# The query graph's product by seven products of halves in place of eight

## The chip, the cores and the metric

The kernel runs on one core of one Trainium2 chip. The metric is the device time of one execution in microseconds (us). The times given are medians of several executions; the profile comes from one more execution.

## The reference

There are 16 batches of x, each with N = 1024 nodes and C = 256 channels, in float32, and one adjacency matrix of 1024 x 1024 that all batches share. Two layers are computed for each batch. What matters here is the first one:

```python
c_adj = mean over channels of x                     # one number for each node
A     = abs(abs(sigmoid(c_j - c_i) - 0.5) - 0.5) * 2
Wg    = adj * (A + A.T) / 2                         # [N, N], other for each batch
g     = x.T @ Wg                                    # [C, N] = [C, N] @ [N, N]: the query graph's product
q     = relu(g * para)                              # queries
kv    = x @ kv_w                                    # keys and values
out   = softmax(q @ k.T * scale) @ v                # four heads of 64 channels
x     = layernorm(x + out)
```

The second layer is a graph convolution of two steps with the plain `adj` (hidden size 128), added to x with a relu and normalised again.

## The kernel before

The order of the work is written out by hand in `run()`; each engine carries out its own instructions in that order, and semaphores join the engines. Batches are staggered. While the attention of batch b is computed, the second layer of batch b-1 (`conv`) and the preparation of batch b+1 are put between its parts.

The attention of a batch has four units (two pairs of heads, two halves of the nodes). In a unit, `scores` makes eight score tiles on TensorE (L388), ScalarE takes their exponential (L391), VectorE adds the eight up for the denominators (L395, L397), transposes the sum and reduces it (L399, L401). `outputs` multiplies with the values (L408) and VectorE transposes the result to `o` (L412). `add` folds the denominators on TensorE (`den_ps`, L420) and divides and adds on VectorE (L424 to L431).

After unit 0 stands `first` (conv.first on TensorE, loads and transposes of x of the next batch, its means), after unit 1 `second` (conv.second, L550), after unit 2 `last` (conv.last, L557 and L558, with a residual sum on VectorE, L562 and L565). In `first` the hidden nodes go through DRAM (`h1d`, L526 and L528).

The queries of batch b+1 are made by the class `Queries`. A batch has eight tiles of 128 rows of Wg. `load` fetches a tile of adj through SP's queue (L334). `likeness` makes A's tile on ScalarE in two activations (L343, L344). `times_adj` multiplies it by adj on VectorE (L349), which gives `wg`. `step(t)` (L357) multiplies the 128 rows of x by the 128 rows of wg: two blocks of channels (cb) by two halves of the nodes (j), four products of 128x128 by 128x512, accumulated over the eight steps in two PSUM tiles of two banks each. TensorE carries out each such float32 product as two passes, which are what the profile counts. `end` multiplies by `para` on VectorE (L363) and applies relu on ScalarE (L364).

After unit 3 stand the eight steps, with parts of the layer norm of batch b among them (`norm.mean`, L265 and L268; `norm.squares`, L274 and L275; `norm.variance`, L279, with a power on GpSimd, L281). Then follow `end`, `norm.scale` (L286), `norm.spread` (two transposes, L174, and eight writes x1d and one load x1 on SP's queue, L295 and L297), `keys` (L307, two halves with a copy on ScalarE each, L309) and `values` (L319, four pieces with a copy each, L321). Then the next batch's scores begin, and the loads of x (L94) and of xB, x in transposed blocks (L106), follow on SP's queue.

Row tiles of 128x1024 come from one pool of 21 buffers. PSUM has three tiles of two banks ("big": scores, g_ps, k_ps, conv) and two of one bank ("bank": av, den_ps, sums, v_ps).

Batch 0's queries are made ahead of the loop, batch 1's during the attention of batch 0, when there is no conv yet.

Of the kernel before, what the change touches and what calls it, by code (L numbers as in the profile page):

```python
# [10 lines left out]
F32 = mybir.dt.float32  # L11
I32 = mybir.dt.int32
AF = mybir.ActivationFunctionType
# [5 lines left out]
def kernel(  # L19
# [31 lines left out]
    nc = tc.nc  # L51

    B, N, C = x.shape
    P = 128
    NT = N // P
    NC = C // P
# [3 lines left out]
    FB = 512  # L60
# [22 lines left out]
    def big_psum(name):  # L83
        return psum.tile([P, N], F32, tag="big", name=name, bufs=3)
# [4 lines left out]
    def bank_psum(name):  # L89
        return psum.tile([P, FB], F32, tag="bank", name=name, bufs=2)  # L90
# [6 lines left out]
    def row_tile(name):  # L97
        return work.tile([P, N], F32, tag="row", name=name, bufs=ROWS)
# [63 lines left out]
    def adj_blocked(mt):  # L162
        t = row_tile(f"adjB_{mt}")
        for a in range(Q):
            nc.sync.dma_start(
                out=t[a * S:(a + 1) * S, :].rearrange("k (bn r) -> k bn r", r=S),
                in_=adj[:, mt * P + a * S:mt * P + (a + 1) * S].rearrange("(bn k) r -> k bn r", k=S))
        return t
# [88 lines left out]
    class BlockedNorm:  # L257


        def __init__(self, xB, sums, name):  # L260
            self.xB, self.sums, self.name = xB, sums, name
# [37 lines left out]
    def keys(b, xT, between=lambda: None):  # L299
        kT = work.tile([P, NC, N], F32, tag="kT", name=f"kT_{b}")  # L300
        for kb in range(NC):
            if kb == 1:
                between()
            pk = big_psum(f"k_ps_{b}_{kb}")
            for j in range(NJ):
                for cc in range(NC):
                    nc.tensor.matmul(pk[:, ts(j, FB)], kvw_sb[:, cc, ts(kb, P)], xT[:, cc, ts(j, FB)],  # L307
                                     start=(cc == 0), stop=(cc == NC - 1))
            nc.scalar.copy(kT[:, kb, :], pk)  # L309
        return kT  # L310

    def values(b, xT, copy=nc.scalar.copy):
        v = work.tile([P, NT, C], F32, tag="v", name=f"v_{b}")
        per = FB // C
        for g in range(NT // per):
            pv = bank_psum(f"v_ps_{b}_{g}")
            for i in range(per):
                for cc in range(NC):
                    nc.tensor.matmul(pv[:, ts(i, C)], xT[:, cc, ts(g * per + i, P)], kvw_sb[:, cc, C:2 * C],  # L319
                                     start=(cc == 0), stop=(cc == NC - 1))  # L320
            copy(v[:, g * per:(g + 1) * per, :], pv.rearrange("p (i c) -> p i c", c=C))  # L321
        return v

    class Queries:
# [26 lines left out]
        def step(self, t):  # L351
            if t == 0:
                self.pg = [big_psum(f"g_ps_{self.b}_{cb}") for cb in range(NC)]
            wg = self.wg.pop(t)
            for cb in range(NC):
                for j in range(NJ):
                    nc.tensor.matmul(self.pg[cb][:, ts(j, FB)], self.xb[:, t, ts(cb, P)], wg[:, ts(j, FB)],  # L357
                                     start=(t == 0), stop=(t == NT - 1))

        def end(self):  # L360
# [3 lines left out]
                nc.scalar.activation(qT[:, cb, :], qT[:, cb, :], AF.Relu, scale=QSCALE)  # L364
            return qT

    class Attention:


# [235 lines left out]
    def run():  # L605

        xT, c_col = prepare_first(x_first)
        q = Queries(0, x_first)
        for t in range(NT):
            q.load(t)
        load_para()
        blocked = load_blocked(1, "1")
        load_weights()

        def first_weights():  # L620
            q.c_row, q.c_col = first_row(c_col), c_col
            q.weigh(0)

        kT = keys(0, xT, first_weights)
        for t in (1, 2):
            q.likeness(t)
        v = values(0, xT, nc.vector.tensor_copy)
        for t in (1, 2):
            q.times_adj(t)
        xb = load_x(1, "1")  # L630
        tiles = {}

        def turn_adj(mts):
            for mt in mts:
                nc.vector.transpose(adjT_sb[:, mt, :], tiles.pop(mt))

        for t in range(NT):
            if t + 3 < NT:
                q.weigh(t + 3)
            q.step(t)  # L640
            if t == 4:
                xB = load_blocked(0, "a0")
                ready = {}
                ready["xT"], ready["part"] = prepare(blocked, "1")
            if t == 6:
                ready["mean"] = means(ready["part"], "1")
        qT = q.end()
        old = conv = None
        for b in range(B):
            more = b + 1 < B  # L650
            att = Attention(b, xB, qT, kT, v)
            if conv and more:
                xb = load_x(b + 1, str(b + 1))

            def first():
                blocked = load_blocked(b + 1, str(b + 1))
                conv.first(blocks=True)
                if old:
                    old.moments()
                conv.turn_blocks(0)  # L660
                ready["xT"], ready["part"] = prepare(blocked, str(b + 1))
                if old:
                    old.finish(out[b - 2])
                conv.turn_blocks(1)
                att.add(0)
                ready["mean"] = means(ready["part"], str(b + 1))

            def second():
                for t in range(3):
                    q.load(t)  # L670
                conv.second(blocks=True)
                att.add(1)

            def last():
                conv.last()
                att.add(2)

            between = [first, second, last] if conv and more else []
            if more:
                q = Queries(b + 1, xb)  # L680
            for u in range(len(UNITS)):
                att.scores(u)
                if u and not between:
                    att.add(u - 1)
                att.outputs(u)
                if u == 2 and more:
                    q.c_row, q.c_col = ready["mean"]
                    for t in range(3):
                        if not conv:
                            q.load(t)  # L690
                        q.weigh(t)
                if u < 3 and between:
                    between[u]()
            norm = BlockedNorm(xB, att.sums, str(b))
            if more:
                xT = ready["xT"]
                for t in range(3, NT):
                    q.load(t)
                for t in range(3, NT):
                    q.likeness(t)  # L700
                if not conv:
                    for mt in range(0, 4):
                        tiles[mt] = adj_blocked(mt)
                q.times_adj(3)
                q.step(0)
                if conv:
                    att.add(3)
                q.times_adj(4)
                q.step(1)
                if not conv:  # L710
                    att.add(3)
                    turn_adj(range(0, 4))
                    for mt in range(4, NT):
                        tiles[mt] = adj_blocked(mt)
                q.times_adj(5)
                q.step(2)
                q.step(3)
                norm.mean()
                q.times_adj(6)
                q.times_adj(7)  # L720
                q.step(4)
                norm.squares()
                q.step(5)
                q.step(6)
                norm.variance()
                xB = load_blocked(b + 1, f"a{b + 1}")
                q.step(7)
                qT = q.end()
                norm.scale()
                norm.spread()  # L730
                if not conv:
                    turn_adj(range(4, NT))
                kT, v = keys(b + 1, xT), values(b + 1, xT)
            else:
                conv.first(lambda: att.add(3))
                norm.mean()
                norm.squares()
                conv.turn(1)
                conv.neighbours(0)
                norm.variance()  # L740
                conv.neighbours(1)
                norm.scale()
                norm.spread()
                conv.last()
                for k, c in ((b - 2, old), (b - 1, conv)):
                    c.moments()
                    c.finish(out[k])
            old, conv = conv, GraphConv(b, norm.x1, norm.x1T)
        conv.first()
        conv.second()  # L750
        conv.ending(out[B - 1])
# [65 lines left out]
```

## Time and profile before

| what | value |
|---|---|
| median of 10 runs | 2298.79 us (2298.13 to 2299.43) |
| the profiled execution's own time | 2298.55 us |
| its span in the profile | 2296.7 us |
| TensorE busy | 2275.7 us (99%), 8422 passes |
| VectorE busy | 1568.3 us (68%) |
| ScalarE busy | 941.3 us (41%) |
| GpSimd busy | 119.2 us (5%) |
| query graph's passes (L357) | 1024, 598 ns mean |
| distance of the scores of neighbouring batches (579.13 and 720.87 us) | 141.7 us |

The span lies 1.85 us below the execution's own time, which is what the runs measure. Engines: PE is TensorE, DVE is VectorE, ACT is ScalarE, POOL is GpSimd, SP is the engine that issues the transfers. A row of the timeline gives start, duration, engine, line, operation, output and inputs, shape and count; after it, in brackets, the idle time of the engine before it and what ended that. A row of the groups gives line, engine, operation, names, shapes and count, then busy time, mean duration in ns, and the idle time before. TensorE's passes overlap, so that their mean duration (598 ns) is longer than the distance at which they follow each other (0.43 us).

### The profile page before, as it was taken

To read this page: it belongs to the slowest core of one execution; us is meant where nothing else is said; L and a number is where in the kernel's file an instruction comes from. 1 tells how busy PE (TensorE), PEld (TensorE's weight loads), DVE (VectorE), ACT (ScalarE), POOL (GpSimd) and SP (SyncE) were. 2 spreads that over 40 slices of the span, in tenths; PEclk is the share of its full clock that TensorE was granted. 3 is DMA by queue.
4 is the path that set the end of the run, shared out by engine and by line. 5 is a ranking of instruction groups with operands and counts; after the bars stand their busy time and mean duration, and the time that the engine had idled before them with its cause. 6 is when DMAs were issued, how large, how long until landed. Compare 5 with 4: busy or idle time off the path is not lost.

```text
span 2296.7 us, 22441 instructions
## 1 busy us (share of the span) xinstructions
PE 2275.7 (99%) x8422; PEld 1089.5 (47%) x8422; DVE 1568.3 (68%) x2055; ACT 941.3 (41%) x1012; POOL 119.2 (5%) x48
## 2 busy tenths in 40 slices
PE   9999999999999999999999999999999999999997
PEld 4354454544445444454444544445444454444454
DVE  4975767567675766757668576685766867667755
ACT  4733435244352443534425244252542535324420
POOL 0000000100001000010000100001000010000001
PEclk9999999999999999999999999999999999999999
DMA  7391362423524245242342434324343252422102
GB/s 185 91 148 46 67 136 55 83 65 75 128 62 76 66 82 119 65 74 83 73 110 64 79 94 81 87 65 85 99 81 75 65 103 81 87 70 65 37 14 80
DMA packets 568467, 189.37 MB, mean 82 GB/s; under 512 B 487072, under 2 KB 551456, under 8 KB 568352
## 3 DMA queue, kind: packets, MB, share of 16 engines
q1 hardware_dynamic: 568080, 187.35, 37.2%
q8 instruction: 68, 1.11, 0.2%
q10 hardware_dynamic: 272, 0.52, 0.1%
q14 instruction: 47, 0.39, 0.1%
HBM read 146.93 MB, written 40.89 MB: 82 GB/s over the span
## 4 chain that ended last, share of the span: by engine, by line
PE 97%; DVE 1%; DMA 0%; ACT 0%; issue 0%; SPq 0%; POOL 0%; DVEq 0%; ACTq 0%
PE s L388 20%; PE av L408 19%; PE g_ps L357 19%; PE h_ps L514 10%; PE u_ps L550 10%; PE v_ps L319 5%; PE k_ps L307 5%; PE t_ps L500 3%; PE h_ps L512 2%; PE h_ps L557 2%; PE h_ps L558 2%; PE sum_ps L214 0%; PE den_ps L420 0%; PE mean_ps L214 0%; DVE acc L397 0%
## 5 line engine op out<-in xcount | busy, mean ns | idle before, releaser
L391 ACT ACTIVATE pr<-s 128x1024 f32<-128x1024 f32 x512 | 476.1, 1052 | 169.6 <-PE s L388 169.6
L397 DVE TENSOR_TENSOR acc<-acc,pr 128x1024 f32<-128x1024 f32 x384 | 470.5, 1225 | 41.0 <-DVE acc L397 1.4
L388 PE MATMUL s<-qT,kT 64*128 64x512 f32 x2048 | 457.1, 596 | 0.7 <-ACT qT L364 0.7
L357 PE MATMUL g_ps<-wg,x 128*128 128x512 f32 x1024 | 455.1, 598 | 1.1 <-DVE wg L349 1.1
L408 PE MATMUL av<-pr,v 128*64 128x512 f32 x2048 | 453.6, 595 | 0.0
L388 PEld LDWEIGHTS s<-qT,kT 64*128 64x128 f32 x2048 | 191.3, 186 | 225.9 <-ACT pr L391 113.6
L357 PEld LDWEIGHTS g_ps<-wg,x 128*128 128x128 f32 x1024 | 189.6, 190 | 229.2 <-issue 222.3
L408 PEld LDWEIGHTS av<-pr,v 128*64 128x64 f32 x2048 | 141.4, 137 | 300.1 <-issue 261.7
L514 PE MATMUL h_ps<-adjT_sb,t 128*128 128x512 f32 x512 | 224.9, 592 | 0.0
L550 PE MATMUL u_ps<-adjT_sb,h 128*128 128x512 f32 x512 | 224.5, 596 | 0.2 <-ACT h L536 0.2
L395 DVE TENSOR_TENSOR acc<-pr,pr 128x1024 f32<-128x1024 f32 x64 | 78.0, 1219 | 152.0 <-ACT pr L391 152.0
L281 POOL TENSOR_TENSOR rstd<-rstd,neg_half 128x32 f32<-128x32 f32 x16 | 86.9, 5429 | 1680.1 <-DVE rstd L279 1680.1
L550 PEld LDWEIGHTS u_ps<-adjT_sb,h 128*128 128x128 f32 x512 | 95.8, 190 | 126.4 <-issue 125.2
L514 PEld LDWEIGHTS h_ps<-adjT_sb,t 128*128 128x128 f32 x512 | 97.2, 190 | 122.5 <-issue 118.3
L349 DVE SCALAR_TENSOR_TENSOR wg<-wg,adj 128x1024 f32<-128x1024 f32 x128 | 149.5, 1209 | 6.1 <-ACT wg L344 6.1
L343 ACT ACTIVATE wg<-c_row,c_col 128x1024 f32<-128x1024 f32 x128 | 147.2, 1150 | 1.2 <-DVE accB L399 1.2
L424 DVE RECIPROCAL rden<-den_ps 64x16 f32<-64x16 f32 x128 | 31.8, 248 | 156.1 <-PE den_ps L420 155.2
L344 ACT ACTIVATE wg<-wg 128x1024 f32<-128x1024 f32 x128 | 135.4, 1058 | 4.1
L552 ACT COPY uT<-u_ps 128x512 f32<-128x512 f32 x32 | 18.7, 585 | 288.1 <-PE u_ps L550 288.1
L515 ACT ACTIVATE h1T<-h_ps,b_sb 128x512 f32<-128x512 f32 x32 | 22.0, 687 | 247.0 <-PE h_ps L514 247.0
L319 PE MATMUL v_ps<-kvw_sb,xT 128*128 128x256 f32 x512 | 113.1, 379 | 0.0
L307 PE MATMUL k_ps<-xT,kvw_sb 128*128 128x512 f32 x256 | 112.8, 593 | 0.0
(101 smaller groups left out, 1786.7 us busy)
## 6 DMA issues: line engine op xcount, KB each, us to landing
adj<-in_adj_dram SPq DMA_DIRECT2D x128, 512.0 KB, 5.8
xB_a<-in_x_dram SPq DMA_DIRECT2D x128, 128.0 KB, 4.0
x1d<-xB_a SPq DMA_DIRECT2D x128, 128.0 KB, 3.4
x<-x1d SPq DMA_DIRECT2D x16, 1024.0 KB, 5.7
xB<-in_x_dram SPq DMA_DIRECT2D x120, 128.0 KB, 4.6
x<-in_x_dram SPq DMA_DIRECT2D x15, 1024.0 KB, 8.7
out_dram<-x SPq DMA_DIRECT2D x15, 1024.0 KB, 4.7
h1d<-h1B SPq DMA_DIRECT2D x112, 64.0 KB, 2.2
```

The lines of the kernel that those rows point to most:

```text
L307: nc.tensor.matmul(pk[:, ts(j, FB)], kvw_sb[:, cc, ts(kb, P)], xT[:, cc, ts(j, FB)], start=(cc == 0), stop=(cc == NC - 1))
L319: nc.tensor.matmul(pv[:, ts(i, C)], xT[:, cc, ts(g * per + i, P)], kvw_sb[:, cc, C:2 * C], start=(cc == 0), stop=(cc == NC - 1))
L343: nc.scalar.activation(wg, self.c_row, AF.Abs, bias=self.c_col[:, t:t + 1], scale=-1.0)
L344: nc.scalar.activation(wg, wg, AF.Tanh, scale=-0.5)
L349: nc.vector.scalar_tensor_tensor(wg, wg, 1.0, self.adj.pop(t), op0=ALU.add, op1=ALU.mult)
L357: nc.tensor.matmul(self.pg[cb][:, ts(j, FB)], self.xb[:, t, ts(cb, P)], wg[:, ts(j, FB)], start=(t == 0), stop=(t == NT - 1))
L388: nc.tensor.matmul(ps[:, ts(s, FB)], self.kT[rows, pair, ts(mt, P)], self.qT[rows, pair, ts(j, FB)], start=True, stop=True)
L391: nc.scalar.activation(pr, ps, AF.Exp)
L397: nc.vector.tensor_add(acc, acc, pr)
L408: nc.tensor.matmul(pav[s * HD:(s + 1) * HD, :], self.v[:, mt, pair * P + s * HD:pair * P + (s + 1) * HD], self.pr[mt][:, ts(s, FB)], start ...
L514: nc.tensor.matmul(ph, t1[:, mt, :], adjT_sb[:, mt, ts(j, FB)], start=False, stop=(mt == NT - 1))
L550: nc.tensor.matmul(pu, self.h1[:, ts(mt, P)], adjT_sb[:, mt, ts(j, FB)], start=(mt == 0), stop=(mt == NT - 1))
```

## The change

For batches 2 to 15 a new class `FastQueries` makes the product with Strassen's algorithm in the form with 15 additions. x is split into 2 x 2 blocks (two blocks of channels by two halves of the rows), Wg into 2 x 2 blocks (two halves of the rows by two halves of the columns). Seven products of blocks, `p[1]` to `p[7]`, replace eight. They are accumulated over four steps, for each of which two tiles of Wg are needed, k and k+4.

- `left`: four sums of blocks of x, 128x512 each, on GpSimd, in `second`.
- `right(k)`: four sums of blocks of Wg, 128x512 each, on VectorE. `pair(k)` is two `times_adj` and `right(k)`.
- `step(k)`: seven products of 128x128 by 128x512. They accumulate in three big PSUM tiles and one bank.
- `end`: a copy of `p[1]` on ScalarE and seven sums of 128x512 on VectorE, then the multiplications by `para` and the relus as before.

The order around it changes too. Tiles 0 and 4 are loaded and weighted and summed in `second`; tiles 1 and 5 after unit 2; tiles 2, 6, 3 and 7 are loaded and their likenesses made after unit 3's scores. `norm.mean` and `norm.squares` stand in the middle of step 2. `norm.variance` stands between the two halves of the keys, `norm.scale` and `norm.spread` between keys and values. For batches 0 and 1 all stays as it was.

The core of the diff; the branch without a conv (`if more and not conv`) keeps its old order:

```diff
+    class FastQueries(Queries):
...
+        def left(self, eng):
+            s12, s34 = (row_tile(f"S_{self.b}_{k}").rearrange("p (s t c) -> p s t c", s=2, c=P) for k in range(2))
+            eng.tensor_add(s12[:, 0], self.block(1, 0), self.block(1, 1))
+            eng.tensor_sub(s12[:, 1], s12[:, 0], self.block(0, 0))
+            eng.tensor_sub(s34[:, 0], self.block(0, 0), self.block(1, 0))
+            eng.tensor_sub(s34[:, 1], self.block(0, 1), s12[:, 1])
+            self.S = [s12[:, 0], s12[:, 1], s34[:, 0], s34[:, 1]]
...
+        def right(self, k):
...
+            nc.vector.tensor_sub(t12[:, h0], lo[:, h1], lo[:, h0])
+            nc.vector.tensor_sub(lo[:, h1], hi[:, h1], lo[:, h1])
+            nc.vector.tensor_sub(t12[:, h1], hi[:, h1], t12[:, h0])
+            nc.vector.tensor_sub(t4, hi[:, h0], t12[:, h1])
...
+        def pair(self, k):
+            self.times_adj(k)
+            self.times_adj(TJ + k)
+            self.right(k)
...
+        def step(self, k, halfway=None):
+            if k == 0:
+                a, b, c = (big_psum(f"g_ps_{self.b}_{i}") for i in range(3))
+                h0, h1 = ts(0, FB), ts(1, FB)
+                self.p = {1: a[:, h0], 6: a[:, h1], 7: b[:, h0], 5: b[:, h1], 2: c[:, h0], 3: c[:, h1],
+                          4: bank_psum(f"g_ps_{self.b}_3")}
...
+            for n in (1, 6, 2, 7, 4, 5, 3) if k == TJ - 1 else (1, 2, 3, 5, 7, 6, 4):
+                if n == 7 and halfway:
+                    halfway()
+                x_n, w_n = terms[n]
+                nc.tensor.matmul(self.p[n], x_n[:, k, :], w_n, start=(k == 0), stop=(k == TJ - 1))
...
+        def end(self):
...
+            nc.scalar.copy(p1, p[1])
+            add(u[:, h0], p1, p[6])
+            add(qT[:, 0, h0], p1, p[2])
+            add(u[:, h1], u[:, h0], p[7])
+            add(qT[:, 1, h0], u[:, h1], p[4])
+            add(qT[:, 1, h1], u[:, h1], p[5])
+            add(u[:, h0], u[:, h0], p[5])
+            add(qT[:, 0, h1], u[:, h0], p[3])
+            for cb in range(NC):
+                nc.vector.tensor_mul(qT[:, cb, :], qT[:, cb, :], para_sb[:, cb, :])
...
             def second():
-                for t in range(3):
+                q.c_row, q.c_col = ready["mean"]
+                q.left(nc.gpsimd)
+                for t in (0, TJ):
                     q.load(t)
+                    q.likeness(t)
+                q.pair(0)
                 conv.second(blocks=True)
                 att.add(1)
...
                 att.scores(u)
+                if u == 3 and more and conv:
+                    for t in (2, TJ + 2, 3, TJ + 3):
+                        q.load(t)
+                    for t in (2, TJ + 2, 3, TJ + 3):
+                        q.likeness(t)
+                    q.right(1)
...
                 if u == 2 and more:
+                    if conv:
+                        for t in (1, TJ + 1):
                             q.load(t)
+                            q.likeness(t)
+                            q.times_adj(t)
...
+            elif more:
+                xT = ready["xT"]
+                q.pair(2)
+                q.step(0)
+                att.add(3)
+                q.pair(3)
+                q.step(1)
+                q.step(2, lambda: (norm.mean(), norm.squares()))
+                q.step(3)
+                qT = q.end()
+                xB = load_blocked(b + 1, f"a{b + 1}")
+                kT = keys(b + 1, xT, norm.variance)
+                norm.scale()
+                norm.spread()
+                v = values(b + 1, xT)
```

More of the change, by code (lines that the diff above doesn't have):

```diff
@@ L365, in end, with __init__, block @@
             return qT
+    class FastQueries(Queries):
+        def __init__(self, b, xb):
+            super().__init__(b, xb)
+            self.T = {}
+        def block(self, i, j):
+            return self.xb[:, j * TJ:(j + 1) * TJ, ts(i, P)]
+        def left(self, eng):
[6 more added lines that the diff above has]
+        def right(self, k):
+            lo, hi = self.wg[k], self.wg[TJ + k]
+            h0, h1 = ts(0, FB), ts(1, FB)
+            t12 = row_tile(f"T_{self.b}_{k}")
+            if k % 2 == 0:
+                self.t4 = row_tile(f"T4_{self.b}_{k}")
+            t4 = self.t4[:, ts(k % 2, FB)]
+            nc.vector.tensor_sub(t12[:, h0], lo[:, h1], lo[:, h0])
+            nc.vector.tensor_sub(lo[:, h1], hi[:, h1], lo[:, h1])
+            nc.vector.tensor_sub(t12[:, h1], hi[:, h1], t12[:, h0])
+            nc.vector.tensor_sub(t4, hi[:, h0], t12[:, h1])
+            self.T[k] = (t12, t4)
+        def pair(self, k):
[5 more added lines that the diff above has]
+                a, b, c = (big_psum(f"g_ps_{self.b}_{i}") for i in range(3))
+                h0, h1 = ts(0, FB), ts(1, FB)
+                self.p = {1: a[:, h0], 6: a[:, h1], 7: b[:, h0], 5: b[:, h1], 2: c[:, h0], 3: c[:, h1],
+                          4: bank_psum(f"g_ps_{self.b}_3")}
+            lo, hi = self.wg.pop(k), self.wg.pop(TJ + k)
+            t12, t4 = self.T.pop(k)
+            h0, h1 = ts(0, FB), ts(1, FB)
+            terms = {1: (self.block(0, 0), lo[:, h0]), 2: (self.block(0, 1), hi[:, h0]), 3: (self.S[3], hi[:, h1]),
+                     4: (self.block(1, 1), t4), 5: (self.S[0], t12[:, h0]), 6: (self.S[1], t12[:, h1]),
+                     7: (self.S[2], lo[:, h1])}
+            for n in (1, 6, 2, 7, 4, 5, 3) if k == TJ - 1 else (1, 2, 3, 5, 7, 6, 4):
[4 more added lines that the diff above has]
+        def end(self):
+            qT = work.tile([P, NC, N], F32, tag="qT", name=f"qT_{self.b}")
+            u = row_tile(f"U_{self.b}")
+            h0, h1 = ts(0, FB), ts(1, FB)
+            p = self.p
+            add = nc.vector.tensor_add
+            p1 = row_tile(f"P1_{self.b}")[:, h0]
+            nc.scalar.copy(p1, p[1])
[8 more added lines that the diff above has]
+                nc.vector.tensor_mul(qT[:, cb, :], qT[:, cb, :], para_sb[:, cb, :])
+                nc.scalar.activation(qT[:, cb, :], qT[:, cb, :], AF.Relu, scale=QSCALE)
+            return qT
@@ L679, in run @@
             if more:
-                q = Queries(b + 1, xb)
+                q = (FastQueries if conv else Queries)(b + 1, xb)
             for u in range(len(UNITS)):
                 att.scores(u)
+                if u == 3 and more and conv:
[4 more added lines that the diff above has]
+                    q.right(1)
                 if u and not between:
@@ L686, in run @@
                 if u == 2 and more:
-                    q.c_row, q.c_col = ready["mean"]
-                    for t in range(3):
-                        if not conv:
+                    if conv:
+                        for t in (1, TJ + 1):
                             q.load(t)
-                        q.weigh(t)
+                            q.likeness(t)
+                            q.times_adj(t)
+                    else:
+                        q.c_row, q.c_col = ready["mean"]
+                        for t in range(3):
+                            q.load(t)
+                            q.weigh(t)
                 if u < 3 and between:
@@ L694, in run @@
             norm = BlockedNorm(xB, att.sums, str(b))
-            if more:
+            if more and not conv:
                 xT = ready["xT"]
@@ L700, in run @@
                     q.likeness(t)
-                if not conv:
-                    for mt in range(0, 4):
-                        tiles[mt] = adj_blocked(mt)
+                for mt in range(4):
+                    tiles[mt] = adj_blocked(mt)
                 q.times_adj(3)
                 q.step(0)
-                if conv:
-                    att.add(3)
                 q.times_adj(4)
                 q.step(1)
[L710 to L714, printed above, removed]
+                att.add(3)
+                turn_adj(range(4))
+                for mt in range(4, NT):
+                    tiles[mt] = adj_blocked(mt)
                 q.times_adj(5)
@@ L730, in run @@
                 norm.spread()
-                if not conv:
-                    turn_adj(range(4, NT))
+                turn_adj(range(4, NT))
                 kT, v = keys(b + 1, xT), values(b + 1, xT)
+            elif more:
+                xT = ready["xT"]
+                q.pair(2)
+                q.step(0)
+                att.add(3)
+                q.pair(3)
[8 more added lines that the diff above has]
+                v = values(b + 1, xT)
             else:
```

## The prediction

> **What bounds the kernel now.** I read the page's shares first, then the chain that ended last, then the timeline of one of the batches that repeat, TensorE's rows and VectorE's.
>
> ```profile
> span 2296.7 us, 22441 instructions
> ...
> PE 2275.7 (99%) x8422; PEld 1089.5 (47%) x8422; DVE 1568.3 (68%) x2055; ACT 941.3 (41%) x1012; POOL 119.2 (5%) x48
> ...
> PEclk9999999999999999999999999999999999999999
> ```
> ```profile
> PE 97%; DVE 1%; DMA 0%; ACT 0%; issue 0%; SPq 0%; POOL 0%; DVEq 0%; ACTq 0%
> ```
> TensorE is busy all through at a steady clock and carries the chain. Only fewer TensorE passes, or new gaps in them, can move the end. In TensorE's timeline (start, duration, count) the changed product stands between two attentions:
> ```profile
> 529.56 7.09 PE L408 MATMUL av<-pr,v 128*64 128x512 f32 x32
> 536.58 3.70 PE L357 MATMUL g_ps<-wg,x 128*128 128x512 f32 x8
> 540.12 0.30 PE L420 MATMUL den_ps<-den_part,fold 128*128 128x32 f32 x2
> 540.26 10.55 PE L357 MATMUL g_ps<-wg,x 128*128 128x512 f32 x24
> 550.64 0.53 PE L214 MATMUL sum_ps<-sums,fold 128*128 128x32 f32 x4
> 551.00 10.55 PE L357 MATMUL g_ps<-wg,x 128*128 128x512 f32 x24
> 561.39 0.53 PE L214 MATMUL sum_ps<-sq_part,fold 128*128 128x32 f32 x4
> 561.75 3.68 PE L357 MATMUL g_ps<-wg,x 128*128 128x512 f32 x8
> 565.27 7.03 PE L307 MATMUL k_ps<-xT,kvw_sb 128*128 128x512 f32 x16
> ```
> No idle time stands in these rows. Row starts (durations overlap) give 540.26 to 550.64 for 24 passes, 0.4325 us each. A product of halves is two passes, 0.865 us; a batch has 32 products, and the stage takes 28.69 us (536.58 to 565.27). VectorE in that stretch:
> ```profile
> 538.17 1.22 DVE L401 TENSOR_REDUCE den_part<-accB 128x32 f32<-128x1024 f32 x1
> ...
> 551.21 0.19 DVE L265 TENSOR_SCALAR mean<-sum_ps 128x32 f32<-128x32 f32 x1 [5.02 <-PE sum_ps L214]
> ...
> 567.75 2.36 DVE L286 TENSOR_TENSOR xB_a<-xB_a,rstd 128x1024 f32<-128x1024 f32 x2 [1.05 <-POOL rstd L281]
> ```
> VectorE is nearly full in attention but idles 5 us and more here, and its timeline shows 10.25 us of idleness in conv.second and 9.89 us ahead of the next scores. The groups give the prices of the new sums:
> ```profile
> L428 DVE TENSOR_TENSOR o<-o,rden 128x512 f32<-128x512 f32 x64 | 43.8, 684 | 0.0
> L562 DVE TENSOR_TENSOR z<-h2e_ps,b_sb 128x512 f32<-128x512 f32 x4 | 2.7, 686 | 17.4 <-PE h2e_ps L558 17.4
> ```
> From SBUF or with a PSUM operand, a 128x512 sum takes 0.69 us. In the timeline the next one starts 0.73 us later if it depends on the first, 0.63 if not; a weighting (L349) starts each 1.14 us.
>
> [...]
>
> **The change, part by part.** It touches the queries of batches 2 to 15: 14 of 16. I put the batch above on a clock with G = 536.58.
>
> (1) TensorE. 28 products in four steps replace 32 in eight: 4 x 0.865 = 3.46 us off the path per batch, 14 x 3.46 = **48.4 us**. Each product loads its own weights, as before; L550, which also changes weights each time, has 32 passes in 13.83 us (0.432 each), so I charge nothing for the new order. The excess of the old stage, 28.69 - 64 x 0.4322 - three short pieces (0.14, 0.36, 0.36) = 0.17, may go too: 2.4 us more at most.
>
> (2) The right-hand sums: 16 of 0.69 us, four per step. One pair of weightings and its sums is 2.28 + 2.76 = 5.04 us. The first pair moves into conv.second: VectorE is free from 632.3 to 643.0, the sums end at 637.4, 5.6 us to spare. Its two adj transfers stand right behind the h1 load on SP's queue (622.4 before), land in 5.8 us, in time for 632.3. Behind the pair stand the adds of unit 1, which wait for den_ps at 642.9 anyway.
> In unit 2 two weightings replace three: VectorE is 0.95 us ahead in unit 3 (the residual then waits for h2_ps). The second adj there waits for the first attention product of unit 2 (650.8), lands near 656.6 and is wanted at 659.5.
> After unit 3's scores, VectorE: L401 ends G+1.8; the sums of step 1 to 4.5; o to 5.1; pair 2 to 10.2; adds of unit 3 (2.8) to 13.0; pair 3 to 18.0. TensorE: step 0 to 6.05, den_ps, step 1 (6.2 to 12.25), step 2 with the mean after its fourth product (at 15.7, sums ready at 13.0), to 18.7; step 3, second product at 19.5 (its sum ready at 17.4), to **24.7**. The closest is 2.1 us. The eight ScalarE likenesses of tiles 2, 6, 3, 7 now begin when accB frees a buffer, G+0.6, and end by 9.4; VectorE wants them from 5.1 (first done 2.8) to 14.2. Their adj land by G+1.4. So the sums cost nothing; without cover they would cost 14 x 11 = 154 us.
>
> (3) Four left sums on GpSimd: [...]13.5 if an add costs four times the 842 ns of the 128x256 row L139. GpSimd reaches them after its pow of the old norm (600.9) and x's load, VectorE then idles until 606.4, and the product needs them 75 us later. I take 0[...].
>
> (4) The end: seven sums and one ScalarE copy (0.59 us, as L552), then the two multiplications as before. Mean, squares and their sums move ahead of it: VectorE 18.0 to 23.0, first sum to 23.7. The keys start at K = G+24.7 and need only that buffer: 1.0 us of room. By the built program the second sum waits for the last product of its shared buffer, K+0.2; the sums start 0.2, 0.83, 1.56, 2.19, 2.82, 3.55. The second key half waits for the one that starts at 2.82, done 3.5; TensorE arrives at 3.46 + 0.36 = 3.82: room **0.3**. The multiplications end at 6.6, ScalarE's relus 7.7, its key copies 9.7, first value copy 10.3; the third value piece wants it at 10.8: room 0.5. Value taken: 0, up to 1.5 us per batch, 21 us, since three of my spacings are 0.1 us guesses.
>
> (5) Variance moves into the keys. Its 0.36 us on TensorE only moves. VectorE's small operation comes after the multiplications (K+6.6), pow takes 5.43, scale starts K+12.2; scores start K+14.2. Scale and the two transposes end 2.8 us after that, the first accumulation is due at 3.15. The cover, 9.89 us of idleness, is used up. The conv wants x1T 14 us into the scores.
> Behind scale on SP stand the eight x1d writes, the x1 load, the x load, eight xB loads: all move 9.6 us later against the scores. The last xB piece landed 16.1 us after the scores' start (issued 591.0, 4.2 us to land); now 25.7. VectorE transposes it at 29.1 and TensorE needs the mean 2.6 us after VectorE has it: room 3.4 + 2.6 = 6.0 us.
>
> Sum against the profiled execution, 2298.55 (span 2296.7 plus 1.85): 2298.55 - 48.4 = 2250.15. The median, 2298.79, lies 0.24 higher; adding that gives 2250.4, and I say **2250.5 us**.
>
> **Rivals.** (A) As worked out: 2247 to 2257, chance 0.74.
> (B) VectorE's chain or the value copies run late where the room is 0.3 to 1.0 us, and TensorE stalls 1 to 2.5 us per batch. For: VectorE is near full from unit 2 to the end, and sums of different operands have not run in this order. Against: every duration is measured. 1.5 us: 2250.4 + 21 = 2271; up to 2285. Chance 0.17.
> (C) The transfers behind scale become the bound: x1d, x1, x and xB follow one another, and in this trace an xB piece took up to 9.5 us to land. From 6.0 us beyond my plan TensorE waits for the mean, from 9.5 us (6.0 + 3.46) the change loses. At 12 us: 14 x 2.5 = 35, 2334. Against: late xB pieces landed in 4 us and nothing else new loads the queues then. Chance 0.05.
> (D) The saving does not happen: seven products take as long as eight, 0.988 us each, since each needs other weights; 2299. L550 speaks against. Chance 0.04.
>
> **Numbers.** A measurement of this kernel tells about 0.2% from no change (4.6 us). Faster is A, B and a rest of D, 0.92; same 0.03; slower C, 0.05. The range 2247 to 2271 goes from the vanished excess to B's likely size and leaves out the rest of B, C and D.
>
> **What would show it.** Right: 912 g_ps passes beside 1024, still 0.432 us apart; the stage near 24.9 us; scores of neighbouring batches near 138.3 us apart, 141.7 before; VectorE busy about 14 x 23 x 0.69 = 222 us more, ScalarE 8. Wrong: idle time of TensorE ahead of k_ps with U as releaser, of v_ps with the value copy (B), of mean_ps with part (C), or g_ps passes above 0.45 us (D).

## The result and the profile after

The changed kernel took 2252.99 us in the median (2252.2 to 2253.71, 8 runs) beside 2299.14 us for the kernel before (28 runs): 46.15 us less, a ratio of 0.980 with a 95% interval of 0.9791 to 0.9808. The profiled execution took 2252.97 us, with a span of 2251.2 us. The prediction was 2250.5 us, in a range of 2247 to 2271.

The page of the changed kernel, its shares, clock and chain:

```profile
span 2251.2 us, 22596 instructions
...
PE 2229.8 (99%) x8310; PEld 1067.3 (47%) x8310; DVE 1773.9 (79%) x2377; ACT 945.4 (42%) x1026; POOL 188.7 (8%) x104
...
PEclk9999999999999999999999999999999999999999
...
PE 97%; DVE 2%; ACT 0%; DMA 0%; issue 0%; SPq 0%; DVEq 0%; POOL 0%; ACTq 0%
```

TensorE has 112 passes less and 46 us less of busy time, and is still busy for 99% of the span. VectorE has gone from 68% to 79% and the chain still runs through TensorE. At the 0.43 us from start to start that a pass takes in the rows below, 112 passes are 48.1 us: the gain is 2 us short of that.

Now TensorE's timeline of one stage (start, duration, engine, line, operation; line numbers are those of the changed kernel). Step 0 begins at 530.45 and the keys at 555.39:

```profile
530.45 1.98 PE L430 MATMUL g_ps<-wg,x 128*128 128x512 f32 x4
532.27 1.02 PE L430 MATMUL g_ps<-wg,S 128*128 128x512 f32 x2
533.13 1.02 PE L430 MATMUL g_ps<-T,S 128*128 128x512 f32 x2
533.99 1.02 PE L430 MATMUL g_ps<-wg,S 128*128 128x512 f32 x2
534.85 1.02 PE L430 MATMUL g_ps<-T,S 128*128 128x512 f32 x2
535.70 1.02 PE L430 MATMUL g_ps<-T,x 128*128 128x512 f32 x2
536.59 0.41 PE L505 MATMUL den_ps<-den_part,fold 128*128 128x32 f32 x2
536.83 1.96 PE L430 MATMUL g_ps<-wg,x 128*128 128x512 f32 x4
...
555.39 3.60 PE L307 MATMUL k_ps<-xT,kvw_sb 128*128 128x512 f32 x8
558.82 0.53 PE L214 MATMUL sum_ps<-sq_part,fold 128*128 128x32 f32 x4
559.18 3.68 PE L307 MATMUL k_ps<-xT,kvw_sb 128*128 128x512 f32 x8
```

The starts of products lie 0.86 us apart, whichever operands they take; the g_ps groups (L430, and L357 for batches 0 and 1) add up to 912 passes, 1024 before. The stage takes 24.94 us, 28.69 before. From the keys to the next scores (569.70) it is 14.31 us, 13.86 before: the variance's piece of 0.36 us has moved there. Together that is 3.30 us a batch, and 14 x 3.30 = 46.2. The scores of neighbouring batches are 138.4 us apart (unit 2 at 495.04 and 633.47), 141.7 before. One row is new in kind: from den_ps's start to the next it is 0.24 us, 0.14 before. VectorE's rows show why:

```profile
516.33 1.23 DVE L647 TENSOR_TENSOR z<-h_ps,b_sb 128x1024 f32<-128x1024 f32 x1 [0.97 <-PE h_ps L643]
...
532.04 1.22 DVE L486 TENSOR_REDUCE den_part<-accB 128x32 f32<-128x1024 f32 x1
...
535.83 0.71 DVE L497 STREAM_TRANSPOSE o<-av 128x512 f32<-128x512 f32 x1
...
548.47 0.69 DVE L405 TENSOR_TENSOR T<-wg,T 128x512 f32<-128x512 f32 x1
549.08 0.18 DVE L265 TENSOR_SCALAR mean<-sum_ps 128x32 f32<-128x32 f32 x1
...
553.96 0.68 DVE L440 TENSOR_TENSOR U<-P,g_ps 128x512 f32<-128x512 f32 x1
...
558.11 0.68 DVE L445 TENSOR_TENSOR U<-U,g_ps 128x512 f32<-128x512 f32 x1
...
567.56 2.36 DVE L286 TENSOR_TENSOR xB_a<-xB_a,rstd 128x1024 f32<-128x1024 f32 x2 [5.56 <-POOL rstd L281]
```

The transpose to o stands behind the four sums of step 1 and ends at 536.54. den_ps may not begin before: `p[4]` holds one of the two single PSUM banks from step 0 to the end, so den_ps has to write the other one, which is av's, the transpose's source. It starts at 536.59, 0.03 us after step 0's last product lets it. Its weight load, which otherwise runs under that product, had to wait too. In the kernel before the products took no single bank, and the first weight load of den_ps began at 539.69, ahead of the end of the transpose to o (539.31 + 0.70):

```profile
539.69 0.19 PEld L420 LDWEIGHTS den_ps<-den_part,fold 128*128 128x128 f32 x1 [0.24 <-DVE den_part L401]
```

In the changed kernel the list of waits has o (what waited, for what, us in total, times, longest). These are idle times of the weight load, which is busy for only 47% of the span (PEld in the page above); the cost is read from the starts above.

```profile
PEld den_ps L505 <- DVE o L497: 9.7, 14, 0.7
```

The 5 us of VectorE's idleness ahead of the mean are used up, since L405 ends at 549.16 and the mean follows at once; the 10.25 us of idleness in conv.second have become 5.70. The groups give the new sums' prices (busy, mean ns, idle time before):

```profile
L402 DVE TENSOR_TENSOR T<-wg 128x512 f32<-128x512 f32 x56 | 38.3, 683 | 0.0
L440 DVE TENSOR_TENSOR U<-P,g_ps 128x512 f32<-128x512 f32 x14 | 9.5, 678 | 0.0
L389 POOL TENSOR_TENSOR S<-x 128x512 f32<-128x512 f32 x14 | 17.7, 1266 | 25.6 <-PE av L493 25.6
```

### The profile page after: what moved, and what is told of

It reads as the page before. It is cut to its first block, busy times and chain, and to the rows that moved or that the text cites. A ratio compares the mean times of both kernels' runs of the same rounds, so it can differ in the third digit from the quotient of the medians.

```text
span 2251.2 us, 22596 instructions
## 1 busy us (share of the span) xinstructions
PE 2229.8 (99%) x8310; PEld 1067.3 (47%) x8310; DVE 1773.9 (79%) x2377; ACT 945.4 (42%) x1026; POOL 188.7 (8%) x104
## 4 chain that ended last, share of the span: by engine, by line
PE 97%; DVE 2%; ACT 0%; DMA 0%; issue 0%; SPq 0%; DVEq 0%; POOL 0%; ACTq 0%
PE s L473 20%; PE av L493 20%; PE g_ps L430 15%; PE h_ps L599 10%; PE u_ps L635 10%; PE k_ps L307 5%; PE v_ps L319 5%; PE t_ps L585 3%; PE h_ps L597 2%; PE h_ps L642 2%; PE h_ps L643 2%; PE g_ps L357 2%; PE den_ps L505 1%; PE sum_ps L214 1%; PE mean_ps L214 0%; DVE acc L482 0%
## 5 line engine op out<-in xcount | busy, mean ns | idle before, releaser
L430 PE MATMUL g_ps<-wg,S 128*128 128x512 f32 x224 | 115.5, 597 | 0.0
L608 DVE STREAM_TRANSPOSE h1B<-h1T 128x512 f32<-128x512 f32 x28 | 19.9, 712 | 121.0 <-ACT h1T L600 121.0
L430 PE MATMUL g_ps<-T,S 128*128 128x512 f32 x224 | 114.4, 592 | 0.0
L430 PE MATMUL g_ps<-wg,x 128*128 128x512 f32 x224 | 110.2, 604 | 0.0
```

The source lines that it names most:

```text
L430: nc.tensor.matmul(self.p[n], x_n[:, k, :], w_n, start=(k == 0), stop=(k == TJ - 1))
```

## The experiments

Three theories stood to be told apart: the number of products alone sets the gain and all else is hidden (1); the sums or the new order cost time that the products paid back (2); TensorE's products or the borders of its pieces cost something else (3). All kernels derive from the changed one. Times are medians of 4 to 13 runs; the kernel before had 2298.3, 2298.96 and 2298.36 us in the three groups of four, and the changed kernel 2252.33 and 2253.07 us in the last two (e5 and e12).

**e1, eight products with all the sums.**

```diff
-            for n in (1, 6, 2, 7, 4, 5, 3) if k == TJ - 1 else (1, 2, 3, 5, 7, 6, 4):
...
-                nc.tensor.matmul(self.p[n], x_n[:, k, :], w_n, start=(k == 0), stop=(k == TJ - 1))
+            for i, wg in enumerate(ws):
...
+                for cb in range(NC):
+                    for j in range(NJ):
+                        nc.tensor.matmul(self.pg[cb][:, ts(j, FB)], self.xb[:, k + i * TJ, ts(cb, P)], wg[:, ts(j, FB)],
+                                         start=(k == 0 and i == 0), stop=(k == TJ - 1 and i == 1))
...
```

`ws` holds the tiles k and k+4, and one sum of `right` goes to another buffer, so that these tiles stay as they are.

> The changed kernel's whole order and all its sums, but the product is the plain one of eight products a step pair again (32 a batch), so the sums feed nothing. Theory 1 (only the number of products counts, the sums and the new order are hidden): the changed kernel's 2253 plus 14 x 4 x 0.86 = 48, so 2301, and 2 us above the kernel before. Theory 2 (the sums or the new order cost time which the seven products had to pay back first): clearly above 2305. Theory 3 (a product costs more in the new order, with other weights each time): below 2297.

Measured: 2329.33 us, ratio 1.0135 (1.0119 to 1.015), 28 us above theory 1. TensorE's timeline of e1 shows where (the bracket is idle time and what ended it):

```profile
540.50 7.13 PE L423 MATMUL g_ps<-wg,x 128*128 128x512 f32 x16
...
568.75 3.60 PE L307 MATMUL k_ps<-xT,kvw_sb 128*128 128x512 f32 x8
572.18 0.53 PE L214 MATMUL sum_ps<-sq_part,fold 128*128 128x32 f32 x4
574.43 5.40 PE L307 MATMUL k_ps<-xT,kvw_sb 128*128 128x512 f32 x8 [1.72 <-DVE qT L442]
```

The stage takes 28.25 us, 3.31 more than with seven products: four products (3.44 us) without the 0.13 us that den_ps waits in the changed kernel, as theory 1 has it. But in e1 the seven sums at the end stand ahead of the multiplications that free the buffer of the second key half, and that wait is 1.9 us a batch (from 572.54, 0.36 us after sum_ps as elsewhere, to 574.43), 26 us in 14. It is a fault of how e1 was built, and it needed another run.

**e6, the same with the seven sums behind the multiplications.**

```diff
+                nc.vector.tensor_mul(qT[:, cb, :], self.pg[cb], para_sb[:, cb, :])
...
+            for n in range(7):
+                add(u[:, ts(n % 2, FB)], p1, p1)
```

> Eight plain products again with the whole new order and all block sums unused, but the seven sums of the end stand behind the multiplications and take their operands from SBUF, so they no longer keep the buffer that the second half of the keys waits for (in e1 TensorE waited 1.7 us for it). Theory 1 (28 products less are 48 us, the sums cost only the 0.13 us wait of den_ps): 2299 to 2302. Theory 2 (the new order costs more elsewhere): above 2305.

Measured: 2299.1 us, ratio 1.0002 (0.9993 to 1.001). As many sums on VectorE and GpSimd and the whole new order, without the saving, cost at most 0.1%. Two things e6 doesn't test: the seven sums in their own place at the end (e8 does), and den_ps's wait. Eight products take no single bank, and den_ps follows step 0 with no gap:

```profile
536.57 7.13 PE L423 MATMUL g_ps<-wg,x 128*128 128x512 f32 x16
543.54 0.30 PE L493 MATMUL den_ps<-den_part,fold 128*128 128x32 f32 x2
543.68 10.55 PE L423 MATMUL g_ps<-wg,x 128*128 128x512 f32 x24
```

Beside it on the same chip the changed kernel took 2252.33 us: four products less a batch, with den_ps's wait against them, are 46.8 us. Theory 2 falls but for that wait.

**e2, seven products without the sums of blocks.**

```diff
+            self.S = [self.block(0, 0), self.block(0, 1), self.block(1, 0), self.block(1, 1)]
+            self.T[k] = (lo, hi[:, h0])
```

> Seven products a step as in the changed kernel, but the sums of blocks (16 on VectorE and 4 on GpSimd a batch) are left out, so the products take raw blocks; the seven sums at the end stay. Theory 1 (sums hidden, but the missing 2 us come from the den_ps matmul that waits for o behind the sums of step 1): 2251 to 2252, and den_ps follows step 0 without a gap. Theory 2 (the sums cost more at several places): 2245 or below. Theory 3 (the missing 2 us are TensorE's own, at the borders of pieces): 2253.

This kernel leaves the sums out, so its queries are not the reference's; only its time is of use. Measured: 2250.68 us, ratio 0.9794 (0.978 to 0.9807), just below theory 1's span. Its timeline of TensorE:

```profile
529.38 6.28 PE L417 MATMUL g_ps<-wg,x 128*128 128x512 f32 x14
535.49 0.30 PE L492 MATMUL den_ps<-den_part,fold 128*128 128x32 f32 x2
535.63 9.69 PE L417 MATMUL g_ps<-wg,x 128*128 128x512 f32 x22
...
554.19 3.60 PE L307 MATMUL k_ps<-xT,kvw_sb 128*128 128x512 f32 x8
```

The stage takes 24.81 us where the changed kernel's takes 24.94, and den_ps has no gap. So the 20 sums of blocks cost 0.13 us a batch.

**e4 and e11, o ahead of the sums of step 1.**

```diff
-                    q.right(1)
...
                 att.outputs(u)
+                if u == 3 and more and conv:
+                    q.right(1)
```

> One move: the sums of step 1 stand behind the transpose of unit 3's outputs to o, so den_ps need not wait for them. Theory 1 (den_ps waits 0.1 us a batch for o): 2251 to 2252, den_ps close behind step 0. Theory 3 (the missing 2 us lie at the borders of pieces): 2253. Were the sums of step 1 late by the move: above 2254.

> The sums of step 1 behind the transpose to o, as in e4, beside the changed kernel on one chip. Theory 1 (den_ps's wait is worth 0.13 us a batch, 1.8 us): 2250.5 to 2251.5, 1 to 2 us below e12. Theory 3 (e4 was scatter): equal to e12.

> The changed kernel on the same chip as e11, as its base: 2252 to 2253.

Measured: e4 2251.09 us, ratio 0.9793 (0.978 to 0.9807). On one chip e11 took 2250.91 us (2250.21 to 2251.16), ratio 0.9792 (0.9779 to 0.9806), and e12 2253.07 us (2252.73 to 2253.78), ratio 0.9802 (0.9789 to 0.9816). The two ratios' intervals overlap, but of the five runs of each the slowest of e11 lies below the fastest of e12. In e4's timeline of TensorE den_ps follows step 0 with no gap:

```profile
535.48 1.02 PE L430 MATMUL g_ps<-T,x 128*128 128x512 f32 x2
536.34 0.30 PE L505 MATMUL den_ps<-den_part,fold 128*128 128x32 f32 x2
536.48 1.96 PE L430 MATMUL g_ps<-wg,x 128*128 128x512 f32 x4
```

Its stage takes 24.81 us (530.22 to 555.03), as without any sums of blocks. So the wait of den_ps for o is the 0.13 us, 1.8 us in 14 batches, of the 2.2 us measured. This version is faster than the changed kernel by 0.1%.

**e3, the left sums on VectorE.**

```diff
-                q.left(nc.gpsimd)
+                q.left(nc.vector)
```

> The four left sums on VectorE in place of GpSimd, at the same place (ahead of the first pair, in conv.second): 4 x 0.69 = 2.8 us into 5.7 us of idleness. Theory 1: 2253, no change. Theory 2 (VectorE has no room there and GpSimd's help is needed): 14 x up to 2.8 us more, 2260 to 2292.

Measured: 2253.78 us, ratio 0.9805 (0.9791 to 0.9818). Theory 1 holds: VectorE's idleness in conv.second falls from 5.70 to 3.18 us, and TensorE's only new wait is one of 0.7 us in all, three times, ahead of den_ps. GpSimd isn't needed for the gain.

**e5, the changed kernel again.**

> The changed kernel once more, as a base beside the other runs of this call: 2253, ratio to the kernel before 0.980.

Measured: 2252.33 us, ratio 0.9798 (0.9785 to 0.9811).

**e7, two more sums in each pair.**

```diff
             nc.vector.tensor_sub(t4, hi[:, h0], t12[:, h1])
+            nc.vector.tensor_sub(t4, hi[:, h0], t12[:, h1])
+            nc.vector.tensor_sub(t4, hi[:, h0], t12[:, h1])
```

> Two more sums of 128x512 in each pair (the last one repeated, same result). Theory 1 (VectorE has 1.8 us of room ahead of the sixth product of step 3): three pairs lie ahead of it, 6 x 0.66 = 4.0 us, so TensorE waits about 2.2 us a batch, 31 us, 2284, with the wait in g_ps. Theory 2 (VectorE has more room, the order gives way): 2253 to 2260. Theory 3 (VectorE's whole added time comes through): 14 x 8 x 0.66 = 74, 2327.

Measured: 2322.43 us, ratio 1.0104 (1.0088 to 1.0119), slower than the kernel before. Theories 1 and 2 are off; theory 3's 2327 is near by accident, since only part of the added time comes through, at two places that no theory named, and a lower clock adds the rest. TensorE's timeline of e7:

```profile
546.61 1.02 PE L432 MATMUL g_ps<-T,x 128*128 128x512 f32 x2
549.30 0.41 PE L507 MATMUL den_ps<-den_part,fold 128*128 128x32 f32 x2 [1.67 <-DVE o L499]
...
567.24 1.02 PE L432 MATMUL g_ps<-wg,S 128*128 128x512 f32 x2
570.30 3.70 PE L307 MATMUL k_ps<-xT,kvw_sb 128*128 128x512 f32 x8 [2.04 <-DVE U L442]
...
712.49 5.40 PE L307 MATMUL k_ps<-xT,kvw_sb 128*128 128x512 f32 x8 [2.04 <-DVE U L442]
```

The sums of step 1's pair alone hold den_ps back, and those of the next two pairs hold back the first sum of the end, which frees the first key half's buffer. No product of step 3 waits. By the starts of the rows den_ps comes 1.4 to 1.8 us late and the first key half 2.2 us, some 53 us in 14 batches. The last row shows a further cost: after the idle time of 2.04 us the eight passes took 5.40 us instead of 3.70, and so in 9 of 14 batches, 15 us. The two make 68 of the 70 us that e7 lies above e5. The mean granted clock was 0.991, 0.998 in the changed kernel; the last section has it for a fast and a slow batch.

**e8, two more sums at the end.**

```diff
             add(qT[:, 1, h1], u[:, h1], p[5])
+            add(qT[:, 1, h1], u[:, h1], p[5])
+            add(qT[:, 1, h1], u[:, h1], p[5])
             add(u[:, h0], u[:, h0], p[5])
```

> Two more sums at the end (the fifth one repeated, same result), ahead of the one that frees the buffer of the second key half: 1.2 to 1.4 us later. Theory 1 (room of 0.3 to 0.4 us): TensorE waits 0.9 to 1.0 us ahead of k_ps, 14 us, 2267; the value copies behind add a little, up to 2275. Theory 2 (the release is not near the path): 2253.

Measured: 2268.9 us, ratio 0.9869 (0.9854 to 0.9884), 16.6 us above e5. Theory 1 holds:

```profile
561.75 0.53 PE L214 MATMUL sum_ps<-sq_part,fold 128*128 128x32 f32 x4
563.22 3.70 PE L307 MATMUL k_ps<-xT,kvw_sb 128*128 128x512 f32 x8 [0.94 <-DVE U L447]
```

Without the wait the second key half would start at 562.11; it starts 1.11 us later, 15.5 us in 14 batches. Of the 1.4 us added, 0.3 were free.

**e9 and e10, more writes on SP's queue.**

```diff
+            for n in range(1):
+                more = dram.tile([N, C], F32, ...)
+                for cc in range(NC):
+                    for a in range(Q):
+                        c0 = cc * P + a * S
+                        nc.sync.dma_start(out=more[:, c0:c0 + S]..., in_=by_node(self.xB[cc][a * S:(a + 1) * S, :]))
             nc.sync.dma_start(out=self.x1, in_=nodes...)
```

e10 has `range(2)`.

> The changed kernel with the eight x1d writes of each norm.spread issued once more, to another DRAM tile that nothing reads, ahead of the x1 load on SP's queue. An issue takes 0.79 us, so the last one ends 6.3 us later, and the x1 load, which waited 2.8 us for the writes to land, starts 3.5 us later, with the x and xB loads behind it. Theory 1 (6.0 us of room in the chain scale, x1d, x1, x, xB before TensorE waits for the mean): 2252 to 2254. Theory 2 (the room is below 3 us): 2260 or more.

> The same with two more sets of eight writes: the x1 load starts about 9.9 us later. Theory 1 (6.0 us of room): TensorE waits 3.9 us a batch ahead of mean_ps, 55 us, about 2307, more where TensorE's clock falls after the gap. Theory 2 (other waits hide more than that): below 2290.

Measured: e9 2255.07 us, ratio 0.9813 (0.9799 to 0.9826), 2 us above e12; e10 2375.15 us, ratio 1.033 (1.0316 to 1.0344). The writes cost more time on the queue than expected. In e9 the x1 load starts 14.7 us after the first x1d write (568.48 to 583.17), 9.15 in the changed kernel: 5.5 us later. The waits of TensorE, of e9 and of e10 (what waited, for what, us in total, times, longest):

```profile
PE mean_ps L214 <- DVE part L207: 2.5, 5, 0.7
```
```profile
PE mean_ps L214 <- DVE part L207: 90.5, 26, 8.1
```

At 5.5 us the mean begins to come late, in some batches and by under 0.7 us: the room of 6.0 us was sized right. In e10 the x1 load starts 12.9 us later, and TensorE waits 90.5 us in all. Its profiled span is 2380.8 us, 129.6 above the changed kernel's; of the rest, 38.5 us are TensorE's busy time, 2268.3 us for the same 8310 passes at a mean granted clock of 0.975, 0.998 in the changed kernel's profile.

## Why the prediction was right

**The step that made the gain.** Part (1) held: 28 products replaced 32, the passes kept their distance, and e6 against e5 gives 46.8 us for them, with den_ps's wait of 1.8 us taken off. Rival D, products that cost more with other weights, is out. The rate was a little high: 0.4325 us a pass was read from stretches with a border in them; products in the middle lie 0.859 us apart, so four are 3.44 us, 48.1 us in all.

**What was missed.** Of the 2 us between 48.1 and 46.15, 1.8 are in part (2). Its schedule has den_ps follow step 0 at once and "o to 5.1", and it did not ask what den_ps waits for. It waits for o, because `p[4]` takes the single bank that den_ps had before; that follows from the program's two banks and the rows above, and no run changed the bank alone. By the prediction's own times o would have been done 0.9 us ahead; it ended at G+6.09, just as den_ps was due. The term behind this was "VectorE is 0.95 us ahead in unit 3": the first residual did run earlier, but the second waited 0.97 us for h2_ps (row L647 above), so nothing was gained. The prediction names that wait itself, and still carries the 0.95 us on: VectorE's entries from L401 (now L486) to pair 3 came 0.7 to 1.0 us later than worked out. The cost is 0.03 us of start and 0.10 us of weight load by the rows, 0.13 us by e2 and e4. With the rate (0.3 us) and a kernel before that this time measured 0.35 us longer, the distance from 2250.5 to 2252.99 is accounted for. The 2.4 us for the old stage's excess, allowed in the range, did not come.

**What was hidden.** Part (2)'s claim that the sums cost nothing, but for this wait, is shown by e2, e4 and e6. VectorE's busy time rose by 205.6 us, not 222, since the rows of neighbouring instructions overlap (one sum starts at 533.89 and takes 0.69 us, the next starts at 534.50). Part (3): the 13.5 us for four sums on GpSimd were an estimate from the 842 ns of one row of L139; an add took 1.27 us (row L389 above), the four 5.1 us. They ran in VectorE's idleness (591.3 to 596.4), and e3 shows that nothing hung on the choice of engine. Part (4)'s room of 0.3 us ahead of the second key half is confirmed by e8, where all but 0.3 us of the added time came through. Part (5)'s room of 6.0 us for the transfers is confirmed by e9.

**The rivals.** B did not happen, but it was near: e7 and e8 show it at two and at two more sums. Its place in e7 was not the product of step 3 but den_ps and the first key half, where there was 0 and 0.75 us of room (U ends 554.64, keys start 555.39). I had put the closest point of part (2) at 2.1 us, and the room at the first key half at 1.0 us in part (4). C is real: with the x1 load 12.9 us later (e10) the kernel was 3% slower. By the prediction's 6.0 us of room TensorE would wait 14 x 6.9 = 97 us; the 90.5 us fit, and the lower clock (0.975 in the mean) came on top. The 9.5 us in C for an xB piece are those of one batch; elsewhere in the trace of the kernel before, one took up to 11.5 us to land.

## What to carry to other kernels

Where one engine carries the whole chain, count the passes that go, at the distance between starts, and then spend the effort on every small operation of that engine in the stage: a piece of 0.14 us between two large ones has waits of its own (0.13 us a batch here), and a new tile in a pool of two banks changes what the others wait for. Room has to be worked out at each place where the bound engine waits, from the end of the releasing instruction; an average of idle time on the other engines (21% of VectorE here) doesn't show that two sums more per pair lose the whole gain.

## What the runs showed of the hardware

In some batches a short gap cost more than its length. In e7 TensorE was idle for 2.04 us ahead of the first key half in each of 14 batches; in nine of them the next eight passes then took 5.40 us, in five 3.70. In e1, with 1.72 us of idleness at the second key half, two of 14 were slow in the same way; in e8, with 0.94 us, none. Here are a fast and a slow batch of e7 (stretch, its length, busy us and instructions of PE, PEld, DVE, ACT and POOL, then the granted clock, the DMA share and GB/s):

```profile
570.30:574.00 3.70, 3.69 (x11) 1.78 (x11) 3.63 (x6) 0.00 (x0) 0.00 (x0) 1.00 0.00 0
712.49:717.90 5.41, 5.41 (x11) 2.39 (x11) 5.31 (x8) 0.33 (x1) 0.00 (x0) 0.68 0.00 0
```

The mean clock is 1.00 in the first stretch and 0.68 in the second: 5.41 us at 0.68 are as much as 3.68 us at 1.00, and the fast batch took 3.70. By this estimate the lower clock accounts for the whole difference. The clock of e1, read in stretches of 200 us (the last of 250), is 0.99 in the two with a slow batch and 1.00 in the nine others.

A gap's length alone does not tell which batches were hit, since gaps of 2.04 us, and of 1.72 us, were followed by a slow stretch in some batches and not in others. The gaps ahead of den_ps in e7, 1.3 us of idleness in 12 batches and 1.67 in two, slowed nothing: the four passes behind den_ps reached the next row after 1.79 to 1.80 us in all 14, 1.80 in the changed kernel (536.83 to 538.63). No run moved or stretched a gap, so what decides it is not shown.
